# One folded product and one reciprocal for the softmax denominators of an image, and row reads of 8 KB

## The chip, the cores and the metric

The kernel runs on one core of a Trainium2 chip. The time is device time in microseconds from the first to the last instruction, as the median of several executions. One further execution was recorded by the hardware profiler, and all views of the profile are of that one.

Engines are named as in the profile: PE is TensorE, DVE is VectorE, ACT is ScalarE, POOL is GpSimd, SP is SyncE, which here issues nearly all DMAs. Each of them works through its own list of instructions in a fixed order; a wait at one instruction holds everything behind it on that engine. "PE" in the profile counts each of this kernel's matmuls twice, since each 32-bit product is recorded as two.

## What is computed

Two layers over x with 8 images, 512 channels and 32 x 32 = 1024 positions, all in 32-bit floats. The first is attention with 8 heads of 64 channels and a residual sum, the second a non-local block and a normalization over all images:

```python
q = conv1x1(x, Wq, bq); k = conv1x1(x, Wk, bk); v = conv1x1(x, Wv, bv)   # per head: 64 x 1024
attn = softmax(einsum('bhdn,bhdm->bhnm', q, k) * d ** -0.5, axis=-1)
x = x + conv1x1(einsum('bhnm,bhdm->bhdn', attn, v), Wp, bp)
...
g, theta, phi = conv1x1(x, g_w), conv1x1(x, theta_w), conv1x1(x, phi_w)
f = einsum('bcn,bdn->bcd', theta, phi) / n
z = conv1x1(einsum('bcd,bdn->bcn', f, g), W_w, W_b) + x
out = batch_normalize(z) * gamma + beta       # mean and variance over images and positions
```

The kernel computes the softmax as an exponential without a shift, a product with v, and a division by the sum of the exponentials over all 1024 keys m. The change is about that sum, the denominator: one number for each head and position, 8 x 1024 for an image.

## The kernel before, in words

**Stages.** All images go through the same stages, one after the other on TensorE: attention of image b, then q, v and k of image b+1, then the projection pp, theta and phi (ptp), g (pg), f (pf), and the product pz of image b. While TensorE computes q, v and k of the next image, VectorE finishes the denominators of the present one. The large products use seven block products in place of eight (`seven`; differences of blocks such as t1 to t4 are their operands), and q, k and pp nest the same scheme once more for two of the blocks, with results in pq_in_s, pk_in_s and pp_in_s; these are emptied one at a time by short sums on VectorE (q, k or x at L298) before their bank is used again. The last image has a shape of its own: there is no next image, so g of image 6, its f and part of its pz lie between attention and projection of image 7, and all results of earlier images are loaded back for the final normalization.

**Attention.** An image has 8 units, each a pair of heads and a half of the positions (`units`), and each unit has 8 steps, one for each block of 128 keys. A step computes scores into a bank (ps, L423), exponentials (e, L426, ScalarE), a running sum over the steps (acc, L430 and L432, VectorE: 128 key rows by 2 heads x 512 positions), and the product with v (po, L449), which lags by two steps.

**Folding.** At the end of a unit the 128 rows of acc still have to be summed. `spread` copies acc in four quarters of 32 rows into the four planes of a tile `fold` (128 x 4 x 1024), at the partitions of this unit: a group of four units fills all 128 partitions, so that three sums of 128 x 1024 (`fold_parts`, L478) reduce four units from 128 to 32 rows each. The three sums for units 0 to 3 are in the middle of attention, those for units 4 to 7 are filled in between matmuls of the next image's q (`fills` in `seven`: after its 6th, 8th and 10th matmul). There are two groups g, each in a tile of its own.

**Denominators.** `denominators(g, ps)` multiplies the folded rows by a matrix `folds` of zeros and ones (128 x 64): two matmuls (L396, one for each head of the pair) sum the 32 rows and leave each sum on 16 equal rows of a bank. A reciprocal over 128 x 512 goes back into the fold tile (L486), and all of it, 256 KB, is written to a DRAM tile den_d (L488). `normalize` reads one row of each 16 back (L497), spread to 64 partitions: four DMAs of 512 KB into a tile r. It has the same buffer as the fold tile, so it can only be filled when that has been read. Four products (L503) then scale o, in the order half by half, and within it group by group.

**Order.** The scheduler of the framework orders each engine's instructions by its own estimate, except those that the code pins in program order (`pe`, `dve`, `sp`): all matmuls, the v sums, the products with r, the fold sums of the second group, the row reads. In the seven images with a successor the order on VectorE after the q stage is: two q sums, reciprocal of group 0, two maxima of q (peak_q, L365), reciprocal of group 1, three v sums, four products with r, and then, mixed, k sums and the differences t_o (L202) that the projection uses. For the eighth image the first group's denominators are computed within attention (at step 46) and the second group's between products of g of image 6; there, `near_end` computes differences t1 to t4 of the held image 6, and calls `midway` between t2 and t3, in which `spread` copies and folds the last unit.

Of the kernel before, what the change touches and what calls it, by code (L numbers as in the profile page):

```python
# [30 lines left out]
def unshifted(ctx: ExitStack, tc: tile.TileContext, a: dict, out: bass.AP):  # L31
# [161 lines left out]
        more_sums(data, which, **how)  # L193
        return data

    def more_sums(data, which, pin=lambda ins: None, midway=lambda: None):
        for i in which:
            l, r = {1: ("12", "11"), 2: ("22", "t1"), 3: ("22", "12"), 4: ("21", "t2")}[i]
            if i == 3:
                midway()  # L200
            data[f"t{i}"] = block(f"t{i}_{data['name']}")
            pin(nc.vector.tensor_tensor(data[f"t{i}"], data[l], data[r], ALU.subtract))  # L202

# [43 lines left out]
    def seven(name, w, data, positions_out, first, add, between=None, early=False,  # L247
              by_chunk=False, inner=None, fills=()):

        nk, half = w.shape[2], w.shape[3]
        tags = list(free)
        free[:] = [tags[3], tags[1], tags[0], tags[2]] if early else [tags[3], tags[1], tags[2], tags[0]]
        slots, begun = {}, set()
        steps, done = iter(()), 0
        if inner:
            free[:] = [tags[1], tags[2], tags[3], tags[0]]
            steps = nested(name, inner, w, data, tags[2:], first, add)
        for n, (what, wi, di, s, reads) in enumerate(FIVE if inner else EARLY if early else SEVEN):  # L260
            if s not in slots or early and what == "t4":
                slots[s] = bank(tags[s], f"{name}_{s}_{n}")
                begun -= {one for one in begun if one[0] == s}
            ps, d = slots[s], data[di]
            if positions_out:
                parts = [(ps.rearrange("p h (i f) -> p (h i) f", f=half)[:, i, :], i * half // 512,
                          lambda k, i=i: d[:, k, i * P:(i + 1) * P], lambda k: w[:, wi, k, :])
                         for i in range(512 // P)]
            else:
                parts = [(ps[:, m, :], m, lambda k, m=m: w[:, wi, k, m * P:(m + 1) * P], lambda k: d[:, k, :])  # L270
                         for m in range(half // P)]
            work = [(*part, k) for part in parts for k in range(nk)]
            if by_chunk and n == 0:
                work.sort(key=lambda one: one[4])
            for to_ps, at, lhsT, rhs, k in work:
                pe(nc.tensor.matmul(to_ps, lhsT(k), rhs(k), start=(s, at) not in begun, stop=(k == nk - 1),  # L276
                                    skip_group_check=True))
                begun.add((s, at))
                if n:
                    next(steps, None)  # L280
                    done += 1
                    if done in (6, 8, 10) and fills:
                        fills[done // 2 - 3]()
            for to, is_first in reads:
                (first if is_first else add)(to, ps)
            if between and n in between:
                between[n]()
# [12 lines left out]


    xt = xp.tile([P, CC, N], F32, tag="x", name="x_0")
    warm = const.tile([P, P], F32, tag="warm", name="warm")
    nc.vector.memset(warm, 0.0)
    _, w_first = weights_tile("WqT", C // 2)
    loaded.append((queue.pop(0), w_first))
    corner["WqT"] = block("a21_WqT")[:, :, :C // 2]
# [7 lines left out]
        nc.scalar.dma_start(to[:, c0:c1], quarter("WqT", m, k)[:, c0:c1])  # L315
    ps = next_bank("warm_ps")[:, 0, :]
    for i in range(WARM):
        pe(nc.tensor.matmul(ps[:, :P], warm, warm, start=True, stop=True))
    bq, bk = load_col("bq", nc.scalar), load_col("bk", nc.scalar)
    load_w(nc.sync)  # L320

# [6 lines left out]
    nc.vector.memset(folds, 0.0)  # L328
    for i in range(4):
        nc.vector.memset(folds[i * P // 4:(i + 1) * P // 4, i * D // 4:(i + 1) * D // 4], 1.0)  # L330
    heads = const.tile([P, P], F32, tag="heads", name="heads")
    nc.vector.memset(heads, 0.0)
    for j in range(2):
        nc.vector.memset(heads[j * D:(j + 1) * D, j * D:(j + 1) * D], 1.0)
    mv = const.tile([P, CC, 2], F32, tag="mv", name="mv")
# [62 lines left out]
    def attention(b, q, k, v, near_end, make_f=None):  # L398
# [7 lines left out]
        units = [(p, h) for p in range(NPAIR) for h in range(NH)]  # L406
        steps = [(u, m) for u in range(len(units)) for m in range(NB)]
        es, accs, sums, folded, o = {}, {}, {}, {}, {}
        tags = list(free)

        def part(u):
# [3 lines left out]
        def scores(i):  # L415
            u, m = steps[i]
            p, h = units[u]
            ps = bank(tags[(0, 1, 3)[i] if i < 3 else (i + 1) % 2], f"ps_{b}_{u}_{m}")
            for j in range(2):
                r = slice(j * D, (j + 1) * D)  # L420
                for c in range(2):
                    keys = slice(m * P + c * P // 2, m * P + (c + 1) * P // 2)
                    pe(nc.tensor.matmul(ps[c * P // 2:(c + 1) * P // 2, j, :], k[r, p, keys],  # L423
                                        q[r, p, h * 512:(h + 1) * 512], start=True, stop=True, skip_group_check=True))
            e = block(f"e_{b}_{u}_{m}")
            nc.scalar.activation(e, ps, AF.Exp, scale=SCALE)  # L426
            es[u, m] = e
            if m == 1:
                accs[u] = w3.tile([P, 2, 512], F32, tag="acc", name=f"acc_{b}_{u}")
                nc.vector.tensor_tensor(accs[u], es[u, 0], e, ALU.add)  # L430
            elif m > 1:
                ins = nc.vector.tensor_tensor(accs[u], accs[u], e, ALU.add)  # L432
                if i == len(steps) - 1 and not make_f:
                    dve(ins)
            if m == NB - 1 and u == len(units) - 1 and make_f:
                near_end(lambda: spread(u, dve))
            elif m == NB - 1:
                spread(u)

# [16 lines left out]
                if i == len(steps) - 1 and not make_f:  # L456
                    dve(ins)

        def spread(u, pin=lambda ins: None):

            g, i = divmod(u, 4)
            if i == 0:
# [4 lines left out]
                eng.dma_start(folded[g][i * P // 4:(i + 1) * P // 4, k, :], acc[k * P // 4:(k + 1) * P // 4, :])  # L467
            if i == 3:
                t = folded[g]
                if g == 1 and not make_f:  # L470
                    return
                if g == 0:
                    folded[g] = fold1.tile([P, 1, 1024], F32, tag="fold1", name=f"fold1_{b}")
                for part_of in fold_parts(g, t, pin):
                    part_of()

        def fold_parts(g, t, pin):
            return [lambda to=to, l=l, r=r: pin(nc.vector.tensor_tensor(to, l, r, ALU.add)) for to, l, r in (  # L478
                (t[:, 0], t[:, 0], t[:, 1]), (t[:, 2], t[:, 2], t[:, 3]), (folded[g][:, 0], t[:, 0], t[:, 2]))]

        def denominators(g, ps):

            t = folded.pop(g)
            columns(ps, folds, lambda j: t[:, 0, j * 512:(j + 1) * 512])
            ri = t[:, 0, :512]
            nc.vector.reciprocal(ri, ps)  # L486
            d = dram2.tile([P, 512], F32, tag="den", name=f"den_d_{b}_{g}")
            nc.sync.dma_start(d, ri)  # L488
            return d

        def normalize(d):

            r = foldp.tile([P, 8, 512], F32, tag="fold", name=f"r_{b}")
            for g in range(2):
                for j in range(2):
                    rows_of = d[g].rearrange("(j i s) n -> j s i n", j=2, i=4)[j, 0]
                    sp(nc.sync.dma_start(r[j * D:(j + 1) * D, 4 * g:4 * g + 4, :], rows_of.partition_broadcast(D)))  # L497

            def products():
                for h in range(NH):  # L500
                    for g in range(2):
                        at = o["o"][:, 2 * g:2 * g + 2, h * 512:(h + 1) * 512]
                        dve(nc.vector.tensor_tensor(at, at, r[:, 4 * g + h:4 * g + 4:2, :], ALU.mult))  # L503

# [2 lines left out]
        for i in range(len(steps) + LAG):  # L507
            if i < len(steps):
                scores(i)
            if make_f and i == 2:  # L510
                make_f(bank(tags[2], f"pf_{b - 1}"))
            if not make_f and i == len(steps) - 2:
                near_end()
            if i >= LAG:
                weighted(i - LAG)
# [2 lines left out]
        free[:] = tags  # L518
        if make_f:
            return o["o"], lambda ps: denominators(1, ps), lambda d: normalize((first_den, d)), None  # L520
        return o["o"], denominators, normalize, fold_parts(1, folded[1], dve)

    def project(b, xt, o, w, between, data=None):
        def first(q, ps):
# [11 lines left out]
    def theta_phi(b, w, data, between):  # L536
# [8 lines left out]
        def first(q, ps):  # L545
            ins = nc.vector.tensor_tensor(at(q), as_tp(ps), tpb[:, int(q[0]) - 1].to_broadcast([P, NB // 2, CI]),
                                          ALU.add)
            if q == "11":
# [1 line left out]

        seven(f"ptp_{b}", w, data, True, first,
              lambda q, ps: nc.vector.tensor_tensor(at(q), at(q), as_tp(ps), ALU.add),
              {0: lambda: more_sums(data, (3, 4), pin=dve), **between})
        return tp

    def make_f(b, tp, ps):
# [81 lines left out]
    def put_away(b):  # L638

        xt, g, wf = late[b]  # L640
        for d in range(IC):
            nc.sync.dma_start(spill_g[b][:, d * N:(d + 1) * N], g[d])
        nc.sync.dma_start(spill_g[b][:, IC * N:], wf)

    def take_back(b):
        t = wr.tile([P, IC * N + IC * C], F32, tag="w", name=f"gwf_{b}")
# [93 lines left out]
    for b in range(B):  # L740
# [2 lines left out]
        if not last:  # L743
            nxt["x"] = load_x(b + 1)

        def near_end(midway=None):
            if last:
                nxt["data"] = data_sums(quarters_of(held["x"]), f"x1_{b - 1}_again", pin=dve, midway=midway)
            else:
                nxt["data"] = data_sums(quarters_of(nxt["x"]), f"x_{b + 1}", (1, 2))  # L750

        def held_f(ps):
            held["f"] = make_f(b - 1, held["tp"], ps)
# [3 lines left out]
        if not last:  # L757
# [2 lines left out]
            q, peak_q = heads_of(b + 1, "q", weights("WqT"), bq, nxt["data"], dve, inner="WqT",  # L760
                                 between={1: lambda: inner_sums(nxt["data"], "t4", dve)}, fills=last_fold)
            load_w(nc.sync)
            d = [denominators(g, next_bank(f"den_{b}_{g}")[:, 0, :]) for g in range(2)]
            v = values(b + 1, weights("WvT"), nxt["data"], {5: normalize(d)})
            load_w(nc.sync)

# [27 lines left out]
        if b == B - LATE:  # L794
            for cc in range(CC):
                nc.sync.dma_start(spill[b][:, cc, :], xt[:, cc, :])
        data = data_sums(quarters_of(xt), f"x1_{b}", (1, 2))
        if last:
            reload_chunks(B - LATE)
        elif b > B - LATE and b != B - 2:  # L800
# [241 lines left out]
```

## Time and profile before

| | us |
|---|---|
| median of 3 executions | 2181.84 (2181.07 to 2182.1) |
| the profiled execution | 2181.89 |
| its span, first to last instruction | 2180.1 |
| mean granted TensorE clock | 0.993 |
| scores ps and product po (L423, L449), on the chain | 20% each |
| ptp, pp, pv, pq, pk, pg (L276), on the chain | 9, 7, 7, 6, 6, 4% |
| denominator products den (L396), 64 records | 15.7 busy |
| reciprocals (L486), 16 of 128 x 512 | 53.6 busy, 3350 ns each |
| fold sums (L478), 48 of 128 x 1024 | 58.7 busy, 1222 ns each |
| VectorE idle before the products with r, for the DMA of r | 36.8 in 8 places |
| copies fold<-acc, 128 KB each, issue to landing | 2.3 median, 2.0 to 4.3 |
| writes den_d<-fold, 256 KB each | 2.5 median |
| reads r<-den_d, 512 KB each | 9.8 median, 5.6 to 15.1 |

The span is the stretch between the first and the last recorded instruction; the execution's own time is 1.8 us longer. Busy times of different engines overlap and don't add up to the span. The chain is what the profiler follows back from the last instruction, at each step to what released it; a share of the chain is a share of the span. In a timeline row the columns are start in us, duration in us (of all instructions merged in the row), engine, line, operation, output<-input with shapes, count, and in brackets the idle time just before and what ended it. In a list of waits they are engine and line, what was waited for, and then us in total, times, and the longest.

### The profile page before, as it was taken

To read this page: it belongs to the slowest core of one execution; us is meant where nothing else is said; L and a number is where in the kernel's file an instruction comes from. 1 tells how busy PE (TensorE), PEld (TensorE's weight loads), DVE (VectorE), ACT (ScalarE), POOL (GpSimd) and SP (SyncE) were. 2 spreads that over 40 slices of the span, in tenths; PEclk is the share of its full clock that TensorE was granted. 3 is DMA by queue.
4 is the path that set the end of the run, shared out by engine and by line. 5 is a ranking of instruction groups with operands and counts; after the bars stand their busy time and mean duration, and the time that the engine had idled before them with its cause. 6 is when DMAs were issued, how large, how long until landed. Compare 5 with 4: busy or idle time off the path is not lost.

```text
span 2180.1 us, 29638 instructions
## 1 busy us (share of the span) xinstructions
PE 2142.0 (98%) x12454; PEld 1109.4 (51%) x12454; DVE 1423.3 (65%) x1612; ACT 741.5 (34%) x848; POOL 45.1 (2%) x50
## 2 busy tenths in 40 slices
PE   9999999999999999999999999999999999999896
PEld 4534663356733566336563366533665346733362
DVE  6477656776477764777747767467673777568626
ACT  1463104631046310562106621165203641065015
POOL 0000100000000000000000000000000000000000
PEclk9999999999999999999999999999999999999998
DMA  6312433124131232313323132231424115111739
GB/s 215 133 38 62 127 150 130 40 66 118 68 131 40 77 108 101 108 40 84 99 93 107 40 103 97 111 81 39 132 99 153 40 30 158 57 40 39 262 127 358
DMA packets 58893, 223.40 MB, mean 102 GB/s; under 512 B 9344, under 2 KB 15744, under 8 KB 53248
## 3 DMA queue, kind: packets, MB, share of 16 engines
q1 hardware_dynamic: 57264, 220.11, 31.8%
q8 instruction: 100, 1.64, 0.3%
q10 hardware_dynamic: 1488, 1.32, 0.2%
q14 instruction: 41, 0.34, 0.0%
HBM read 138.03 MB, written 49.81 MB: 86 GB/s over the span
## 4 chain that ended last, share of the span: by engine, by line
PE 93%; DMA 2%; DVE 2%; issue 1%; ACT 1%; SPq 0%; DVEq 0%
PE ps L423 20%; PE po L449 20%; PE ptp L276 9%; PE pp L276 7%; PE pv L276 7%; PE pq L276 6%; PE pk L276 6%; PE pg L276 4%; PE pf L561 3%; PE pz L276 2%; PE pk_in_s L239 2%; PE pq_in_s L239 2%; PE pp_in_s L239 2%; PE pz L671 2%; DMA r<-den_d 1%; PE pwf L596 1%
## 5 line engine op out<-in xcount | busy, mean ns | idle before, releaser
L426 ACT ACTIVATE e<-ps 128x1024 f32<-128x1024 f32 x512 | 522.9, 1025 | 427.9 <-PE ps L423 422.4
L432 DVE TENSOR_TENSOR acc<-acc,e 128x1024 f32<-128x1024 f32 x384 | 470.0, 1224 | 129.3 <-ACT e L426 121.6
L449 PE MATMUL po<-e,v 64*64 64x512 f32 x4096 | 528.7, 589 | 0.7 <-ACT w_WgT L563 0.7
L423 PE MATMUL ps<-q,k 64*64 64x512 f32 x4096 | 529.1, 589 | 0.0
L449 PEld LDWEIGHTS po<-e,v 64*64 64x64 f32 x4096 | 156.5, 133 | 283.4 <-issue 275.4
L423 PEld LDWEIGHTS ps<-q,k 64*64 64x64 f32 x4096 | 155.6, 133 | 284.1 <-issue 275.0
L584 ACT ACTIVATE g<-pg,gb 128x512 f32<-128x512 f32 x31 | 21.3, 687 | 398.8 <-PE pg L276 395.9
L430 DVE TENSOR_TENSOR acc<-e,e 128x1024 f32<-128x1024 f32 x64 | 78.2, 1222 | 108.7 <-ACT e L426 73.4
L276 PE MATMUL ptp<-w_tp,t_x 128*128 128x256 f32 x512 | 116.7, 384 | 2.4 <-DVE t_x L202 2.4
L276 PE MATMUL pv<-w_WvT,t_x 128*128 128x256 f32 x512 | 114.5, 379 | 0.0
L276 PEld LDWEIGHTS ptp<-w_tp,t_x 128*128 128x128 f32 x512 | 97.8, 192 | 16.1 <-DVE t_x L202 2.9
L276 PEld LDWEIGHTS pv<-w_WvT,t_x 128*128 128x128 f32 x512 | 97.2, 190 | 13.2
L276 PE MATMUL pp<-t_o,w_WpT 128*128 128x512 f32 x208 | 100.9, 592 | 0.0
L276 PE MATMUL pq<-t_x,w_WqT 128*128 128x512 f32 x200 | 98.8, 593 | 0.9 <-DVE w_WqT L723 0.9
L276 PE MATMUL pk<-t_x,w_WkT 128*128 128x512 f32 x200 | 98.9, 592 | 0.0
L379 ACT COPY v<-pv 128x1024 f32<-128x1024 f32 x32 | 32.4, 1012 | 191.2 <-PE pv L276 191.2
L276 PE MATMUL pv<-w_WvT,x 128*128 128x256 f32 x384 | 87.5, 381 | 0.0
L276 PE MATMUL ptp<-w_tp,x 128*128 128x256 f32 x384 | 86.8, 379 | 0.0
L380 DVE TENSOR_TENSOR v<-v,pv 128x1024 f32<-128x1024 f32 x24 | 29.3, 1222 | 79.9 <-PE pv L276 79.9
L276 PEld LDWEIGHTS pv<-w_WvT,x 128*128 128x128 f32 x384 | 72.4, 190 | 15.7 <-issue 5.9
L276 PEld LDWEIGHTS ptp<-w_tp,x 128*128 128x128 f32 x384 | 73.0, 190 | 13.3 <-issue 3.6
L276 PE MATMUL pp<-o,w_WpT 128*128 128x512 f32 x144 | 70.1, 611 | 7.8 <-issue 5.2
(181 smaller groups left out, 2200.4 us busy)
## 6 DMA issues: line engine op xcount, KB each, us to landing
fold<-acc SPq DMA_DIRECT2D x254, 128.0 KB, 2.3
r<-den_d SPq DMA_DIRECT2D x32, 512.0 KB, 9.8
x<-in_x_dram SPq DMA_DIRECT2D x31, 512.0 KB, 6.1
w_WqT<-kept_WqT SPq DMA_DIRECT2D x7, 2176.0 KB, 8.8
w_WkT<-kept_WkT SPq DMA_DIRECT2D x7, 2176.0 KB, 8.3
w_WpT<-kept_WpT SPq DMA_DIRECT2D x6, 2176.0 KB, 8.9
w_WvT<-kept_WvT SPq DMA_DIRECT2D x7, 1792.0 KB, 7.2
w_tp<-kept_tp SPq DMA_DIRECT2D x7, 1792.0 KB, 7.4
```

The lines of the kernel that those rows point to most:

```text
L239: pe(nc.tensor.matmul(ps, a[wi], d[di], start=s not in begun, stop=True, skip_group_check=True))
L276: pe(nc.tensor.matmul(to_ps, lhsT(k), rhs(k), start=(s, at) not in begun, stop=(k == nk - 1), skip_group_check=True))
L379: seven(f"pv_{b}", w, data, True, lambda q, ps: nc.scalar.copy(at(q), as_v(ps)), lambda q, ps: dve(nc.vector.tensor_tensor(at(q), at(q), a ...
L380: lambda q, ps: dve(nc.vector.tensor_tensor(at(q), at(q), as_v(ps), ALU.add)), between)
L423: pe(nc.tensor.matmul(ps[c * P // 2:(c + 1) * P // 2, j, :], k[r, p, keys], q[r, p, h * 512:(h + 1) * 512], start=True, stop=True, skip_gr ...
L426: nc.scalar.activation(e, ps, AF.Exp, scale=SCALE)
L430: nc.vector.tensor_tensor(accs[u], es[u, 0], e, ALU.add)
L432: ins = nc.vector.tensor_tensor(accs[u], accs[u], e, ALU.add)
L449: pe(nc.tensor.matmul(ps[j * D:(j + 1) * D, r, :], v[keys, m, (2 * p + j) * D:(2 * p + j + 1) * D], e[keys, j, :], start=(m == 0), stop=(m ...
L561: pe(nc.tensor.matmul(ps[:, c, :], tp[:, i, c * P:(c + 1) * P], tp[:, i, CI:], start=(i == 0), stop=(i == NB - 1)))
L596: pe(nc.tensor.matmul(ps, f[:, c, d * P:(d + 1) * P], ww[:, c, :], start=(c == 0), stop=(c == IC - 1)))
L671: pe(nc.tensor.matmul(ps[:, h - h0, :], wf[:, d, oc * P:(oc + 1) * P], g[d][:, h * 512:(h + 1) * 512], start=(d == 0), stop=(d == IC - 1), ...
```

## The change

For the seven images with a successor, the three fold sums of the second group stay where they were (`fold_last`: after the 6th, 8th and 10th matmul). With the last of them, four DMAs on SP's queue copy the 32 rows of each unit of both groups into two planes of the fold tile, every other row into each (64 rows of 4 KB a copy), and after the 14th matmul a further sum adds the two planes: all eight units now lie on the 128 partitions with 16 rows each. `all_denominators` needs one product of two matmuls with a new matrix `folds8`, one reciprocal, and one write of 16 rows of 2 KB: one row for each sum. These rows are laid out so that the four rows that a partition of r needs follow each other, 8 KB in one piece.

For the last image the two groups keep their own products and reciprocals. The second reciprocal goes into another tile (`ri`), the rows of group 0 are read as soon as the second product is done, and the writes are of 8 rows each. t1 and t2 of the held image are computed during attention (after steps 59 and 61), t3 and t4 while the last copies of acc are under way.

The products with r now run group by group. In the last image all four differences of x1 are made before ptp. `heads` takes the place of `warm` for the warm-up matmuls and is filled with its ones afterwards; `folds8` is built on GpSimd; for image 6 the writes of `put_away` are pinned in SP's order.

```diff
     def seven(name, w, data, positions_out, first, add, between=None, early=False, by_chunk=False, inner=None, fills=()):
...
-                    if done in (6, 8, 10) and fills:
-                        fills[done // 2 - 3]()
+                    if done in fills:
+                        fills[done]()
...
+    folds8 = const.tile([P, D], F32, tag="folds8", name="folds8")
+    nc.gpsimd.memset(folds8, 0.0)
+    nc.gpsimd.affine_select(out=folds8, in_=folds8, compare_op=ALU.is_gt, fill=1.0, base=1 - P // 8,
+                            pattern=[[-P // 8, 8], [0, D // 8]], channel_multiplier=1)
+    nc.gpsimd.affine_select(out=folds8, in_=folds8, compare_op=ALU.is_ge, fill=0.0, base=0,
+                            pattern=[[-P // 8, 8], [0, D // 8]], channel_multiplier=1)
...
             if m == NB - 1 and u == len(units) - 1 and make_f:
-                near_end(lambda: spread(u, dve))
+                spread(u, dve, near_end)
...
             if i == 3:
                 t = folded[g]
+                meanwhile()
                 if g == 1 and not make_f:
                     return
...
+        def fold_last():
+
+            t = folded.pop(1)
+            folded["all"] = t[:, 1]
+            adds = [lambda to=to, l=l, r=r: dve(nc.vector.tensor_tensor(to, l, r, ALU.add)) for to, l, r in (
+                (t[:, 0], t[:, 0], t[:, 1]), (t[:, 2], t[:, 2], t[:, 3]), (t[:, 0], t[:, 0], t[:, 2]),
+                (t[:, 1], t[:, 1], t[:, 2]))]
+            first = folded.pop(0)[:, 0]
+
+            def last_of_group():
+                adds[2]()
+                for g, rows_32 in enumerate((first, t[:, 0])):
+                    for half in range(2):
+                        nc.sync.dma_start(t[g * D:(g + 1) * D, 1 + half, :],
+                                          rows_32.rearrange("(r s) n -> s r n", s=2)[half])
+
+            return {6: adds[0], 8: adds[1], 10: last_of_group, 14: adds[3]}
...
+        def all_denominators(ps):
+
+            t = folded.pop("all")
+            columns(ps, folds8, lambda j: t[:, j * 512:(j + 1) * 512])
+            ri = t[:, :512]
+            nc.vector.reciprocal(ri, ps)
+            d = dram2.tile([16, 512], F32, tag="den", name=f"den_d_{b}")
+            nc.sync.dma_start(d, ri.rearrange("(a s) n -> a s n", a=16)[:, 0, :])
+            d = d.rearrange("(j g i) n -> g j (i n)", j=2, g=2)
+            return d[0], d[1]
+
         def denominators(g, ps):
...
-            ri = t[:, 0, :512]
+            alone = make_f and g == 1
+            ri = (fold1.tile([P, 1, 1024], F32, tag="fold1", name=f"ri_{b}") if alone else t)[:, 0, :512]
             nc.vector.reciprocal(ri, ps)
-            d = dram2.tile([P, 512], F32, tag="den", name=f"den_d_{b}_{g}")
-            nc.sync.dma_start(d, ri)
-            return d
+            if alone:
+                rows_of(0, first_den)
+            d = dram2.tile([8, 512], F32, tag=f"den{g}", name=f"den_d_{b}_{g}")
+            nc.sync.dma_start(d, ri.rearrange("(a s) n -> a s n", a=8)[:, 0, :])
+            return d.rearrange("(j i) n -> j (i n)", j=2)
+
+        def rows_of(g, d):
+            if "all" not in rows:
+                rows["all"] = foldp.tile([P, 8, 512], F32, tag="fold", name=f"r_{b}")
+            rows[g] = rows["all"][:, 4 * g:4 * g + 4, :].rearrange("q i n -> q (i n)")
+            for j in range(2):
+                sp(nc.sync.dma_start(rows[g][j * D:(j + 1) * D, :], d[j].partition_broadcast(D)))
 
         def normalize(d):
 
-            r = foldp.tile([P, 8, 512], F32, tag="fold", name=f"r_{b}")
             for g in range(2):
-                for j in range(2):
-                    rows_of = d[g].rearrange("(j i s) n -> j s i n", j=2, i=4)[j, 0]
-                    sp(nc.sync.dma_start(r[j * D:(j + 1) * D, 4 * g:4 * g + 4, :], rows_of.partition_broadcast(D)))
+                if g not in rows:
+                    rows_of(g, d[g])
+            r = rows["all"]
 
             def products():
-                for h in range(NH):
-                    for g in range(2):
+                for g in range(2):
+                    for h in range(NH):
...
-            if not make_f and i == len(steps) - 2:
+            if i in ((len(steps) - 5, len(steps) - 3) if make_f else (len(steps) - 2,)):
                 near_end()
...
-            d = [denominators(g, next_bank(f"den_{b}_{g}")[:, 0, :]) for g in range(2)]
+            d = denominators(next_bank(f"den_{b}")[:, 0, :])
...
-        data = data_sums(quarters_of(xt), f"x1_{b}", (1, 2))
+        data = data_sums(quarters_of(xt), f"x1_{b}", (1, 2, 3, 4) if last else (1, 2))
```

## Prediction, made before the changed kernel ran

> **What bounds the kernel.** I read the page's shares and its chain of waits first, then the waits of TensorE alone, then the timeline of the stages that the diff touches.
>
> ```profile
> PE 2142.0 (98%) x12454; PEld 1109.4 (51%) x12454; DVE 1423.3 (65%) x1612; ACT 741.5 (34%) x848; POOL 45.1 (2%) x50
> ...
> PE 93%; DMA 2%; DVE 2%; issue 1%; ACT 1%; SPq 0%; DVEq 0%
> ...
> PE pp L276 <- issue: 5.2, 1, 5.2
> PE pk_in_s L239 <- DVE k L298: 3.0, 2, 2.2
> PE pp L276 <- DVE o L503: 2.6, 1, 2.6
> PE ptp L276 <- DVE t_x L202: 2.4, 1, 2.4
> ```
>
> TensorE is busy for 98% of the span and carries 93% of the chain; its own waits sum to about 16 us. So time comes out in two ways only: fewer matmuls, or fewer of those few waits. VectorE at 65% costs nothing except where TensorE waits for it. Fewer reciprocals are therefore worth nothing by themselves (16 x 3350 ns is all VectorE time), and I look for the waits they feed.
>
> **1. One product for the denominators (seven images).** On the chain each image has its denominators as one piece; the last image shows one group alone.
>
> ```profile
> 480.86 1.87 PE den L396 x8
> ...
> 1982.70 1.01 PE den L396 x4
> ```
>
> Two groups take 1.87 us, one takes 1.01 (x4 is two matmuls, each recorded twice). The new product has the shape of one group: 1.87 - 1.01 = 0.86 us off TensorE, and nothing lies beside it. Seven images: **-6.0 us** (0.78 to 0.93 each, depending on how the first weight load is hidden). The eighth keeps two separate products.
>
> **2. What the product now waits for.** A new round trip stands before it: fold sums, four copies SBUF to SBUF (64 rows of 4 KB, 256 KB each), one more 128x1024 sum, product. In the second image:
>
> ```profile
> 470.67 2.48 DVE L478 TENSOR_TENSOR fold<-fold 128x1024 f32<-128x1024 f32 x2
> 478.40 2.34 DVE L365 TENSOR_REDUCE peak_q<-q 128x1 f32<-128x1024 f32 x2
> 480.79 1.94 PE L396 MATMUL den<-fold,folds 128*64 128x512 f32 x8
> ```
>
> The last sum ends at 473.15. Four issues of about 0.6 us follow on SP, where nothing else waits until the WkT load at 480.89. The trace has no 256 KB copy inside SBUF; its nearest row is fold<-acc, 128 KB in rows of 4 KB: 2.3 us median, 4.3 at most. I take 2.5, so the last copy lands at 477.5 (478.7 at worst). VectorE's static order puts the added sum between the two peak_q reductions. The first starts at 478.40 and the issue interval is 1.13, so the sum runs 479.53 to 480.76. TensorE reaches the product at 480.79: just in time, with a hand-over on top. I charge 0.1 us per image, **+0.7** (0 to 1.5). Behind the waiting sum stand a reduction, two sums that empty a bank of q, and the reciprocal; the bank's next use is late in the v stage, some 17 us on, so their delay of 1.1 us costs nothing. If the copies land after 479.5, every microsecond costs one per image.
>
> **3. The rows come earlier.** Now the second reciprocal starts at 488.63, after two reductions, and the rows are issued at 494.24. With one reciprocal, at 484.1 to 487.4, a 32 KB write in place of two of 256 KB (2.5 us) puts the reads at about 489.9. In most images the late rows are hidden; in the fourth they were not:
>
> ```profile
> 1035.65 1.22 DVE L503 TENSOR_TENSOR o<-o,r 128x1024 f32<-128x1024 f32 x1
> ...
> 1043.10 3.50 DVE L503 TENSOR_TENSOR o<-o,r 128x1024 f32<-128x1024 f32 x3 [6.24 <-DMA r<-den_d]
> ...
> 1046.52 0.41 DVE L298 TENSOR_TENSOR k<-k,pk_in_s 128x256 f32<-128x256 f32 x1
> ...
> 1046.99 0.70 PE L239 MATMUL pk_in_s<-i_x,w_WkT 128*128 128x256 f32 x2 [2.19 <-DVE k L298]
> ```
>
> VectorE sits 6.24 us in its queue for the rows, the k sums behind it are late, and TensorE stops. By the starts on the chain this k stage takes 1037.76 to 1064.12 = 26.36 us, the five others between 23.2 and 23.5 (772.57 to 795.83, for one): 3.1 lost. In the first image it is 238.27 to 264.08 = 25.81, of which 0.81 is the bias product at 263.13: 1.8 lost. The order after puts three t_o differences ahead of the first k sum. From the v sum at 1034.51: eight operations at 1.14 us put the k sum at +9.1, while TensorE needs it at +9.8 (1046.52 - 2.19 - 1034.51). Tight, but clear by 0.7 if the rows are there. In the first image the order also puts weight sums there, which need loads issued when v ends. I take 3.1 whole and 1.4 of 1.8: **-4.5** (2 to 5).
>
> Are the rows there? The old reads landed up to 15.1 us after issue (5.6 to 15.1). 489.9 + 15.1 = 505.0 meets the second group's product, now third in order, at 503.9 + 2.3 - 0.9 = 505.3: enough even with no faster reads. The Trainium skill speaks against the 8 KB rows (*DMA: Bandwidth & Descriptors*, section "Why small descriptors are slow"): the bus overhead is some three cycles per packet. Its arithmetic at 2 KB gives an estimate of 3/67, about 4%, so four times longer packets would leave 15 us at 14.5. The trace says otherwise: while the 2 KB rows run, the window from 496 to 507 has 171 GB/s at a DMA share of 0.86; just before, with the 17 KB rows of a weight, the DMA view shows 429. I lean to the trace, perhaps 8 us, but the sum is the same by both: the earlier issue does the work.
>
> **4. The last image: projection.** Here the rows are waited for openly.
>
> ```profile
> 2028.35 0.33 SPq L488 DMA_DIRECT2D den_d<-fold  x1
> 2030.60 3.75 SPq L497 DMA_DIRECT2D r<-den_d  x4
> 2039.91 1.23 DVE L503 TENSOR_TENSOR o<-o,r 128x1024 f32<-128x1024 f32 x1 [9.00 <-DMA r<-den_d]
> 2041.24 5.88 PE L276 MATMUL pp<-o,w_WpT 128*128 128x512 f32 x8 [5.18 <-issue]
> 2047.16 1.41 DVE L530 SCALAR_TENSOR_TENSOR x<-pp,bp,x 128x512 f32<-128x512 f32 x2 [6.02 <-PE pp L276]
> 2049.76 3.70 PE L276 MATMUL pp<-o,w_WpT 128*128 128x512 f32 x8 [2.63 <-DVE o L503]
> ```
>
> TensorE stops at 2036.06, and its first eight records take 5.88 us instead of the usual 3.6, since the window 2040 to 2050 has a granted clock of 0.72. After: the first group's rows are read as soon as the second product has freed the fold buffer, about 2023.4 (its reciprocal no longer writes into it), and land by 2031 at the old pace. Both first-group products come before the second group's. So pp starts when the matmuls before it end (2035.9, with the 0.2 wait at pwf also gone) and takes 3.5, to 2039.4. Then the order has two x sums ahead of the second group's products: 2 x 0.66 + 1.2, so the second eight still wait 2.6, now to 2041.9 instead of 2049.76: **-7.85**. The second rows are no limit: reciprocal over at 2026.9 (two differences no longer ahead of it), reads at 2029.1, landed by 2037.
>
> That wait of 2.6 may cost clock. The skill (*TensorE: Matmul & The Clock Gate*, section "Why this matters for your kernels") lets idle gaps of up to about 3 us pass free. The trace has 2.63 without a drop and 2.45 (at ptp, below) followed by half clock. I take the row: about one chance in two of losing 1.7, **+0.95**; by the rule nothing.
>
> **5. The last image: ptp.**
>
> ```profile
> 2085.61 1.22 DVE L202 TENSOR_TENSOR t_x<-x 128x1024 f32<-128x1024 f32 x1
> 2086.75 1.22 DVE L202 TENSOR_TENSOR t_x<-x,t_x 128x1024 f32<-128x1024 f32 x1
> 2086.89 5.27 PE L276 MATMUL ptp<-w_tp,t_x 128*128 128x256 f32 x16 [2.45 <-DVE t_x L202]
> 2092.00 3.62 PE L276 MATMUL ptp<-w_tp,x 128*128 128x256 f32 x16
> ```
>
> The differences t3 and t4 move ahead of the tp sums, into the first 3.5 us of ptp. The wait goes, 2.45, and with it the half clock: sixteen records took 5.11 instead of 3.45. **-4.1** by the row (2.45 by the skill's rule). The first tp sum moves from 2074.11 to 2075.4; its bank is wanted at 2077.4. Nothing is late next.
>
> Edits at nothing: t1 and t2 of the held image inside attention (2.3 us of VectorE, which idles 0.49 in each 1.72 us step); POOL's three instructions for folds8 (2% busy); the second memset of heads, behind a weight sum at 8.25 us, long after the warm-up at 4.7. Uncovered, each costs its own length, at most 2.3 once.
>
> **Sum.** -6.0 + 0.7 - 4.5 - 7.85 + 0.95 - 4.1 = -20.8. The profiled execution took 2181.89 us, the median is 2181.84: **2161 us**, 1% faster. Behind this the output tail follows TensorE; weight and spill loads have slack (DMA share 0.74 and 0.50 after 2060).
>
> **Rivals.**
> *The last image gives little* (0.20): another wait takes the place, the first rows land late, or ptp waits elsewhere. For it: four kinds of DMA meet there, and the windows from 2040 to 2060 show a DMA share of 1.02. Against: rows are issued before all of it. -20.8 + 11 leaves -10: 2172.
> *Small waits in every image* (0.10): product or k sum late by 0.5 to 1 us, on the thin margins of 0 and 0.7 us above: 7 x 0.8 = 5.6, 2167.
> *Slower* (0.04): the copies of part 2 land late. They pay from 6.4 us after the sums; 3 us more per image eats all 20.8, so it decides at about 9.4. At 10.4, near the rows' median of 9.8, each image loses 4 us and mostly a half-clock window of 1.7: 7 x 5.7 = 40, 2201. The 2.3 and 4.3 of fold<-acc speak against it.
> *No change* (0.02): the saved matmuls turn into waiting and the last image fails too: about 2180.
> The forecast has 0.64, its own range 2157 to 2165. With the next two: **2156 to 2170**. A measurement tells apart 0.2%, 4.4 us: faster 0.94, same 0.02, slower 0.04.
>
> **What would show it.** Right: den x4 on each image's chain with no wait before it; both k stages near 23.3; no wait for r on VectorE before the last image; pp after pz without a gap, then one of 2.6; no wait at ptp. Wrong: TensorE waiting at den for the fold sum, or at pk_in_s in images that ran clean.

## The result, and the profile after

The changed kernel takes 2171.47 us (median of 6, 2170.06 to 2172.12), the kernel before on the same chip 2182.16 us (median of 6): ratio 0.995, interval 0.9937 to 0.9963. It is faster by 10.7 us, where 20.8 were forecast, and 1.5 us above the range. Small waits in every image, one of the rivals, were what happened, at twice the size given there; their cause, copies that land late, stood under another rival, *Slower*.

The page after, shares and chain, and below it the waits of TensorE alone (engine, line, what for, us in total, times, longest):

```profile
PE 2131.9 (98%) x12426; PEld 1108.3 (51%) x12426; DVE 1411.2 (65%) x1611; ACT 741.6 (34%) x848; POOL 44.1 (2%) x53
...
PE 98%; issue 1%; DVE 1%; ACT 1%
...
PE den L398 <- issue: 11.4, 7, 1.8
PE pp L274 <- DVE o L545: 2.6, 1, 2.6
```

Of the four waits that the prediction lists, only the 2.6 us at pp is left, and one line is new: TensorE waits 11.4 us in seven places for the new product, 1.6 an image. That is the whole distance to the forecast. The view calls it "issue", which only says that it could not name the releaser. The rows of VectorE and SP in the second image show what it was (timeline of the kernel after):

```profile
469.47 4.52 SPq L494 DMA_DIRECT2D fold<-fold  x4
469.69 2.48 DVE L485 TENSOR_TENSOR fold<-fold 128x1024 f32<-128x1024 f32 x2
477.42 1.21 DVE L367 TENSOR_REDUCE peak_q<-q 128x1 f32<-128x1024 f32 x1
480.14 1.23 DVE L485 TENSOR_TENSOR fold<-fold 128x1024 f32<-128x1024 f32 x1 [1.51 <-DMA fold<-fold]
481.47 1.08 PE L398 MATMUL den<-fold,folds 128*64 128x512 f32 x4 [1.58 <-issue]
```

The fold sums end at 472.17 and the copies behind them have landed at 480.14. VectorE was free from 478.63 and TensorE from 479.88. The product follows the added sum by 0.1 us, so its 1.58 us are the copies' lateness, handed on. The data view from 469 to 481 us (columns of 0.3 us; busy share of the DMA engines in tenths, then GB/s) shows why they are late:

```profile
DMA  0000069950000059979987988996998200000009
GB/s 0 0 0 0 0 246 396 164 68 0 0 0 0 0 205 423 177 96 164 137 109 109 191 96 123 137 137 82 150 164 96 27 0 0 0 0 0 0 0 522
```

While the copies run the engines are busy nearly all the time, but after a fast start they move only some 130 GB/s. By the trace's own packets (4 KB each), the quickest quarter takes 156 to 168 ns and the slowest half 458 to 641. It isn't a fixed time to land either: the four copies land 3.8, 4.2, 5.6 and 6.7 us after their issues. The queue is full, and slow.

The rest came as forecast. Both k stages that had lost time now take what the others take (starts on the chain after, first and fourth image; the first has its bias product of 0.79 in it):

```profile
239.10 4.29 PE pk L274 x10
...
263.09 24.14 PE pp L274 x56
...
1039.28 4.29 PE pk L274 x10
...
1062.49 4.29 PE pp L274 x10
```

That is 23.99 and 23.21 us, against 25.81 and 26.36 before.

### The profile page after: what moved, and what is told of

The parts are those of the page before. It is cut to its first block, busy times and chain, and to the rows that moved or that the text cites. A ratio compares the mean times of both kernels' runs of the same rounds, so it can differ in the third digit from the quotient of the medians.

```text
span 2169.5 us, 29636 instructions
## 1 busy us (share of the span) xinstructions
PE 2131.9 (98%) x12426; PEld 1108.3 (51%) x12426; DVE 1411.2 (65%) x1611; ACT 741.6 (34%) x848; POOL 44.1 (2%) x53
## 4 chain that ended last, share of the span: by engine, by line
PE 98%; issue 1%; DVE 1%; ACT 1%
PE ps L426 20%; PE po L452 20%; PE pv L274 9%; PE ptp L274 9%; PE pp L274 7%; PE pq L274 7%; PE pk L274 7%; PE pg L274 4%; PE pf L603 3%; PE pz L274 2%; PE pq_in_s L237 2%; PE pk_in_s L237 2%; PE pp_in_s L237 2%; PE pz L714 2%; PE pwf L638 1%
## 5 line engine op out<-in xcount | busy, mean ns | idle before, releaser
L274 PEld LDWEIGHTS pv<-w_WvT,t_x 128*128 128x128 f32 x512 | 97.2, 190 | 13.2
L274 PEld LDWEIGHTS ptp<-w_tp,x 128*128 128x128 f32 x384 | 73.0, 190 | 13.3 <-issue 3.6
```

## The experiments

All start from the changed kernel. Times are medians, and a ratio is to the kernel before, run beside it. With the short labels below, that kernel took 2179.9 us beside e1, e2, e3 and e4, 2179.5 beside e3b, e5, e7 and b3, and 2177.8 beside e8 and e9, so totals of different groups compare to some 2 us only, and the waits in the traces are the finer measure.

**Fewer bytes at the end (e1).** The copies of group 0 leave earlier, into planes 1 and 3 (`with_copies` makes a sum, then issues the copies that are named).

```diff
-                (t[:, 1], t[:, 1], t[:, 2]))]
+                (t[:, 1], t[:, 1], t[:, 3]))]
...
-            return {6: adds[0], 8: adds[1], 10: last_of_group, 14: adds[3]}
+            return {6: with_copies(0, (0, first, 0)), 8: with_copies(1, (0, first, 1)),
+                    10: with_copies(2, (1, t[:, 0], 0), (1, t[:, 0], 1)), 14: adds[3]}
```

> Only the place of the copies changes: those of group 0 go into planes 1 and 3 of the fold tile right after the 6th and 8th fill, so that after the last fold sum only 512 KB are still to be copied, in place of 768. Theory A (the copies are slow by their bytes, about 131 GB/s): they are over 2 us earlier, the wait of the product falls from 1.6 us to under 0.2 in each of seven images, 7 x 1.5 = 10.5 less than the change: 2161. Theory B (a copy inside SBUF lands a fixed 6 us after its issue): the last copy is still issued after the last sum, only 0.5 us earlier; the wait stays at 1.0 or more: 2167 to 2169.

Measured: 2166.31 us, ratio to before 0.9936 (0.992 to 0.9953). The wait fell to 0.9 us an image (4.4 in five, 2.1 in two), between the two forecasts. Theory B falls, since the copies land 4.2, 4.8, 5.5 and 6.7 us after their issues. Theory A had the rate too high. By the packets of the second image, the two copies of group 1 are under way from 473.28 to 477.70 us, 512 KB at 119 GB/s. And the 256 KB that are no longer at the end would have been the quick ones: of the three last copies of the change the first takes 1.4 us from first to last packet, the other two 2.4 each.

**Same bytes, other partitions (e2).** A copy's rows go to every second partition of all 128; `folds2` is `folds8` with its rows exchanged to match. Theory A1 below is that the destination's partitions set the rate.

```diff
-                        nc.sync.dma_start(t[g * D:(g + 1) * D, 1 + half, :],
+                        nc.sync.dma_start(t[:, 1 + half, :].rearrange("(r g) n -> g r n", g=2)[g],
                                           rows_32.rearrange("(r s) n -> s r n", s=2)[half])
...
+    folds2 = const.tile([P, D], F32, tag="folds2", name="folds2")
+    for g in range(2):
+        nc.sync.dma_start(folds2.rearrange("(r g) n -> g r n", g=2)[g], folds8[g * D:(g + 1) * D, :])
```

> Same four copies, same bytes, same time of issue, but a copy's 64 rows go to every second partition of all 128 instead of to 64 neighbouring ones (the matrix of ones has its rows exchanged to match). Theory A1[...]: 1 MB moves at 250 GB/s or more, the added sum finds its data, no wait at the product: 2161. Theory A2 (the rate belongs to 4 KB rows copied within SBUF, wherever they go) and B (fixed time to land): wait of 1.6 us per image as before, 2171.5.

Measured: 2159.93 us, ratio 0.9905 (0.9888 to 0.9921). No wait at the product. The data view of this run, same window:

```profile
DMA  8930000008999997000000000000000000990367
GB/s 341 410 123 0 0 0 0 0 0 314 396 369 423 410 423 287 0 0 0 0 0 0 0 0 0 0 0 0 0 0 0 0 0 0 519 290 0 116 232 290
```

Some four hundred GB/s, and every 4 KB packet of this image's four copies takes 156 to 176 ns. In the timeline the added sum follows the reduction without idle time, and the product follows q:

```profile
475.86 1.21 DVE L370 TENSOR_REDUCE peak_q<-q 128x1 f32<-128x1024 f32 x1
476.99 1.22 DVE L488 TENSOR_TENSOR fold<-fold 128x1024 f32<-128x1024 f32 x1
478.12 1.21 DVE L370 TENSOR_REDUCE peak_q<-q 128x1 f32<-128x1024 f32 x1
478.31 1.08 PE L401 MATMUL den<-fold,folds 128*64 128x512 f32 x4
```

So the rate, and with it the 11 us, hangs on which partitions the copies touch, and neither on the bytes alone nor on a fixed time: the four copies land after 2.3 to 2.4 us.

**Which side of the copy (e9).** Source rows that are neighbours, destination as in the change. This kernel leaves out the right pairing of rows, so it serves for the times alone.

```diff
-                                          rows_32.rearrange("(r s) n -> s r n", s=2)[half])
+                                          rows_32[half * D:(half + 1) * D])
```

> The copies take 64 neighbouring rows in place of every other one, to 64 neighbouring partitions as in the change; the sums then mix the rows of two units, so the denominators are not those of the reference. Theory A1 (the destination's 64 neighbours set the rate): the copies stay at some 131 GB/s and the product waits 1.6 us. Rival (the source's step of two partitions has a part in it): the rate is clearly other than 131 GB/s; [...]the copies are over 2 us earlier and the wait is under 0.3.

Measured, one execution: 2158.84 us, no wait at the product. The data view, from 468 to 480 us:

```profile
DMA  0000999920000899968999983000000000000099
GB/s 0 0 0 0 218 205 191 191 68 0 0 0 0 205 218 205 177 150 246 355 273 287 259 178 68 0 0 0 0 0 0 0 0 0 0 0 0 0 635 290
```

The median packet takes 316 ns. My theory that the 64 neighbours at the destination alone set the rate has fallen. Three pairs of patterns gave three rates. From first to last packet, the three copies behind the fold sums (768 KB) took in the second image 2.1 us from every second partition to every second (375 GB/s), 3.6 from neighbours to neighbours (221), and 5.5 from every second to neighbours (144, with the fast start). So neighbours on both sides cost two fifths of the rate, and spreading only the source made it worse. The Trainium skill (*SBUF — State Buffer*, section "Door 1: The DMA port swizzle") says that DMA bandwidth depends on how many of 16 ports the partitions reach, and by its formula 64 neighbouring partitions reach 8: an estimate of half of its 436 GB/s, 218. That fits the second pair and not the third, and the measurement decides. What makes the third slower still was not tried, nor was the fourth pair, neighbours to every second.

**The product later (e3, e3b).** TensorE goes on with v first. `make_denominators` holds the product, the reciprocal and the reads; its key says behind which block of v it stands.

```diff
-            d = denominators(next_bank(f"den_{b}")[:, 0, :])
-            v = values(b + 1, weights("WvT"), nxt["data"], {5: normalize(d)})
+            v = values(b + 1, weights("WvT"), nxt["data"], {0: make_denominators, 5: lambda: scale["o"]()})
```

> The copies stay as slow as in the change, but TensorE comes to the product 3.4 us later, after the first block of v. Theory A and B alike: the copies land meanwhile, no wait on TensorE, and the rows still arrive in time: 2171.5 - 7 x 1.6 = 2160.5. Rival (the delay of the added sum on VectorE is what costs, by q sums and banks that come free late): TensorE waits elsewhere in v, and most of the 11 us stays, 2167 to 2171.

Measured: 2171.19 us, ratio 0.9956 (0.9939 to 0.9972): nothing gained. The product waits 1.5 us again, though TensorE now comes to it 3.6 us later:

```profile
480.31 1.22 DVE L485 TENSOR_TENSOR fold<-fold 128x1024 f32<-128x1024 f32 x1 [1.52 <-DMA fold<-fold]
481.45 1.21 DVE L367 TENSOR_REDUCE peak_q<-q 128x1 f32<-128x1024 f32 x1
482.58 2.34 DVE L296 TENSOR_TENSOR q<-q,pq 128x1024 f32<-128x1024 f32 x2
485.02 1.08 PE L398 MATMUL den<-fold,folds 128*64 128x512 f32 x4 [1.53 <-issue]
```

Its data had been there since 481.5. It starts 0.1 us after the two q sums end, which stand behind the late sum on VectorE. By the order in which the code hands out banks (`next_bank`), the product was given, at this place, the bank that they read. The next run moves it one more block on:

```diff
-            v = values(b + 1, weights("WvT"), nxt["data"], {0: make_denominators, 5: lambda: scale["o"]()})
+            v = values(b + 1, weights("WvT"), nxt["data"], {1: make_denominators, 5: lambda: scale["o"]()})
```

> In the run before, TensorE came to the product 3.4 us later and waited all the same, until the q sums that stand behind the added sum on VectorE had emptied the bank that the product was given. Here the product comes one block of v later still, 6.9 us after the end of q, and those sums are over by then. If the bank was the cause: no wait at the product, 2171.5 - 7 x 1.6 = 2160.5. If it is something that moves along with the product, a wait of 1.5 us stays, 2171.

Measured: 2159.94 us, ratio 0.9906 (0.9889 to 0.9923), no wait at the product, though VectorE still stands 10.5 us in seven places for copies as slow as ever. The lateness costs only where TensorE meets it. Slow copies hidden are worth as much as fast ones.

**Two products again (e4).** The seven images as before, with the compact rows and the new order of the products with r.

```diff
-            d = denominators(next_bank(f"den_{b}")[:, 0, :])
+            d = [denominators(g, next_bank(f"den_{b}_{g}")[:, 0, :]) for g in range(2)]
...
-            return {6: adds[0], 8: adds[1], 10: last_of_group, 14: adds[3]}
+            return {6: adds[0], 8: adds[1], 10: adds[2]}
```

> The seven images get two products and two reciprocals again, without copies and added sum; row layout, 8 KB reads, order of the products and the last image stay as changed. If the single product with its wait is a loss as it stands (1.57 + 1.08 = 2.65 us against 1.87): 2171.5 - 7 x 0.78 = 2166, faster than the change. If the 4.5 us that the first and fourth image gained came from the single reciprocal, they return: 2170, with waits at pk_in_s. If they came from faster reads as well, they stay away.

Measured: 2165.12 us, ratio 0.9932 (0.9915 to 0.9949), no wait at pk_in_s. The folding that gives the change its name was a loss of 6 us as it stood, 0.8 an image. And the first and fourth image keep their gain with two reciprocals. An earlier issue is not the reason here: the reads leave 13.0 to 13.2 us after the product starts, before the change 13.3 to 14.3. What differs is that their last packet ends 10.9 to 11.9 us after the first issue, before 14.0 to 16.8, and that the products with r take group 1 third and not second. The two were not tried apart.

**The row reads (e5, e8).** Pieces of 2 KB again, first 4 KB apart, then 32 KB as before the change (the number of rows in den_d and the 2 below become 16 times the written rows and 16).

```diff
-            d = dram2.tile([16, 512], F32, tag="den", name=f"den_d_{b}")
+            d = dram2.tile([32, 512], F32, tag="den", name=f"den_d_{b}")
+            d = d.rearrange("(a s) n -> a s n", s=2)[:, 0, :]
...
-                sp(nc.sync.dma_start(rows[g][j * D:(j + 1) * D, :], d[j].partition_broadcast(D)))
+                sp(nc.sync.dma_start(rows[g][j * D:(j + 1) * D].rearrange("q (i n) -> q i n", i=4), d[j].partition_broadcast(D)))
```

> The changed kernel with the rows of r read in pieces of 2 KB again, as many bytes and DMAs, issued at the same time. Theory of the prediction (the earlier issue does the work, not the size of a piece): the reads may land later than the 6.8 us median of the change, but VectorE meets at most a short wait for them in the last image, and the time stays at 2171.5 within 1.5. Rival (8 KB pieces are what removed the wait): waits for r of some 5 us on VectorE and waits at pk_in_s return, 2174 to 2178.

> The pieces of 2 KB that make up a row of r now lie 32 KB apart in DRAM, as they did before the change (4 KB apart in the run with 2 KB pieces, which read as fast as 8 KB pieces did). If the distance made the old reads slow: median from issue to landing near the 9.8 us of before and a longest one near 15. If it was what else was under way at the time: 7 to 7.5 median, 11 at most, as in the run with 2 KB pieces. Time in both cases 2171.5 within 2.

Measured: 2171.43 us (ratio 0.9958, 0.9941 to 0.9974) with 4 KB between the starts of pieces, 2172.3 in one execution with 32 KB. Shortest, median and longest time of a read from issue to landing, in the kernels before and after and in these two:

| | piece | apart | us |
|---|---|---|---|
| before | 2 KB | 32 KB | 5.6 / 9.8 / 15.1 |
| after | 8 KB | 2 KB | 4.5 / 6.8 / 10.4 |
| first run | 2 KB | 4 KB | 5.0 / 7.2 / 10.7 |
| second run | 2 KB | 32 KB | 5.6 / 8.3 / 15.3 |

(For the kernel after, "apart" is the distance of the rows that make up one piece.) The size of a piece is worth little, 6.8 against 7.2 us; the distance in DRAM carries the long tail. It accounts for the old reads: in the seven images whose four reads leave together, the fourth lands after 12.7 to 15.1 us before the change, 9.8 to 10.4 after it, 10.0 to 10.7 in the first run and 12.5 to 15.3 in the second. (The medians 9.8 and 8.3 differ because the last image of the changed kernels reads two by two.) Neither shows in the time, since the reads now start early enough, 8.5 us after the product in most images: the run with 32 KB has only 2.8 us of waits for r on VectorE in all, and TensorE waits where it does in the change, to 0.4 us.

**The last image, ptp (e7).** t3 and t4 go back behind the tp sums.

```diff
-        data = data_sums(quarters_of(xt), f"x1_{b}", (1, 2, 3, 4) if last else (1, 2))
+        data = data_sums(quarters_of(xt), f"x1_{b}", (1, 2))
```

> The changed kernel with t3 and t4 of x1 in the last image left where they were before, behind the sums of tp. Theory: the wait at ptp comes back, 2.45 us, and if its 3.4 us window of the clock is mostly idle another 1.7: 2174 to 2176. Rival (VectorE is ahead by now and the wait does not return): 2171.5.

Measured: 2174.11 us, ratio 0.9974 (0.9962 to 0.9985), 2.6 above the change. That alone is little more than totals can tell; the trace has the wait again, and this time without half clock:

```profile
2080.83 3.72 PE L274 MATMUL ptp<-w_tp,t_x 128*128 128x256 f32 x16 [2.45 <-DVE t_x L200]
2084.39 3.62 PE L274 MATMUL ptp<-w_tp,x 128*128 128x256 f32 x16
```

Sixteen records take 3.56 us from start to start; before the change, after the same wait of 2.45, they took 5.11.

**The best version (b3).** Copies to every second partition, and in the last image the first x sums of pp behind the products with r.

```diff
-                nc.vector.scalar_tensor_tensor(at, ps[:, m, :], bp[:, c:c + 1], at, ALU.add, ALU.add)
+                ins = nc.vector.scalar_tensor_tensor(at, ps[:, m, :], bp[:, c:c + 1], at, ALU.add, ALU.add)
+                if b == B - 1 and q == "11":
+                    dve(ins)
```

> The copies to every second partition as in the second experiment, and in the last image the two x sums of the first block of pp pinned behind the four products with r. Theory: the wait of 2.6 us at the second block of pp goes, and with it the window at half clock behind it: 2160 - 2.6 - 1.7 = 2155.7. Rival (the second group's rows land later than TensorE needs them, so the wait stays): 2159 to 2160.

Measured: 2156.21 us (2156.05 to 2156.43), ratio 0.989 (0.9874 to 0.9907). The wait at the second block of pp is down to 0.3:

```profile
2027.38 2.36 DVE L548 TENSOR_TENSOR o<-o,r 128x1024 f32<-128x1024 f32 x2 [3.86 <-DMA r<-den_d]
2028.66 3.70 PE L274 MATMUL pp<-o,w_WpT 128*128 128x512 f32 x8 [0.31 <-DVE o L548]
```

VectorE waits 3.86 us for the second group's rows here, and it costs TensorE 0.31, since it falls under the first block. This kernel beats the change by 15 us and the one before by 23.

## Why the prediction was wrong

**The failed step is the second, "what the product now waits for".** It put the last copy's landing at 477.5 us, "478.7 at worst", and charged 0.1 us an image. TensorE reaches the product 0.9 us earlier after the change; by that clock the copies were due at 476.6, and they were there at 480.1. I had taken the landing of one copy of 128 KB and added the time to issue four of 256 KB. (With the row's longest landing of 4.3 us that sum gives 479.3, not 478.7: next to no margin before 479.5.) But the four queue behind each other, and what counts is their sum. Three of them come after the last fold sum: their 768 KB were under way for 5.5 us, with 1.2 us before the first packet and 1.3 behind the last, 8.0 in all; to every second partition the same bytes took 2.1. The row that I called nearest said so in another view: in the trace of before, four copies of 128 KB to 32 partitions each keep the engines at a mean of about 200 GB/s, with a median packet of 307 ns, about twice the shortest of the change. I read the time to landing and not the rate. The skill's page quoted above would have warned at half the rate.

Point by point, with the spans of the two profiled executions (2180.1 and 2169.5 us, 10.6 less):

| step | forecast | measured | from |
|---|---|---|---|
| 1, one product | -6.0 | -5.5 | 7 x (1.08 - 1.87), starts on the chain |
| 2, its wait | +0.7 | +11.4 | the list of waits |
| 3, k stages of two images | -4.5 | -5.0 | -1.8 and -3.15 |
| 4, pp of the last image | -7.85 | -8.3 | pg's start to pp's second block: 35.06 and 26.76 us |
| 4, half clock behind its wait | +0.95 | +1.4 | rest of pp: 20.70 and 22.09 us |
| 5, ptp of the last image | -4.1 | -4.3 | 28.44 and 24.18 us |
| sum | -20.8 | -10.3 | |

- *Step 2, the point of decision.* That a late landing pays from 6.4 us after the sums, one for one in each image, was right. It landed at 7.97.
- *Step 3.* The gain was right and its reason half right. One reciprocal is not needed for it: with two reciprocals and compact rows it stays. "The earlier issue does the work" holds for the run with pieces 32 KB apart, where the reads are as slow as before; the run with two products shows that quicker reads, with the new order of the products, do it too. On the size of a piece I leaned to the trace against the skill's rule of a few cycles a packet, and the rule was nearer: 6.8 and 7.2 us. The slow rate that I had read off came with the distance of 32 KB, which the row did not show.
- *Step 4.* The reordered products and the early reads did what was said: pp starts 20.5 us after pg (21.2 forecast) and its second block 26.8 after it (27.2). The remaining wait, read off the static order, was 2.63. It cost half clock, as charged at one chance in two. The window after it (its length, the busy times of PE, PEld, DVE, ACT and POOL, then granted clock, DMA share and GB/s):

```profile
2041.30:2044.80 3.50, 2.85 (x4) 1.30 (x5) 3.47 (x4) 0.00 (x0) 0.00 (x0) 0.51 0.95 388
```

  The 0.51 is the granted clock. So gaps under 3 us are not always free, against the skill's guideline quoted in the prediction; but the run on ptp shows the same gap of 2.45 without a drop. The traces say when. In all twelve, the stretches of full and half clock within the kernel last whole multiples of 3.41 us. Lay that step over each trace, from some 11 us to the last matmul: half clock follows all 10 steps in which TensorE is idle for 2.00 us or more, and none of the 42 with 1.00 to 1.98. The wait of 2.63 put 2.05 us into one step after the change and, split by a boundary, 1.98 before it; at ptp the 2.45 gave 2.21 before and 1.08 and 1.37 in the run with t3 and t4 back. So the drop here was a matter of where the wait fell: 7 of the 11 traces with this wait have it. This is read off the traces; no run set out to test it.
- *The edits at nothing* cost nothing that shows: no wait of TensorE before the last image other than at the product and two that were there before, 1.1 us at the warm-up matmuls and 0.7 at po.
- *The range* missed because the margin of nothing at the product was known ("just in time") but its bounds were drawn from one narrow row.

## What to carry to other kernels

When copies are put between two steps of a busy engine, price them by what queues together divided by a rate measured for that pattern of partitions, not by the landing of one. Copies within SBUF that touched 64 neighbours ran here at 0.6 or 0.4 of the rate of those that had every second partition on both sides; spread both sides, or give the engine that waits something else to do first, past any bank that the delay holds. An engine that is saved work but made to wait for longer loses: here the halved product lost 6 us until its wait was removed.

## What the runs showed that I had not expected

- 768 KB in 4 KB rows from partition to partition within SBUF, 64 rows a DMA, took 2.1 us from every second partition to every second, 3.6 from neighbours to neighbours and 5.5 from every second to neighbours, with the DMA engines busy nearly all the time in each case (packets of 161, 316 and 458 ns in the median).
- Reads that spread DRAM rows to 64 partitions, four of 512 KB together: the last lands after 10.7 us at most when its pieces of 2 KB start 4 KB apart, and after 12.5 to 15.3 when they start 32 KB apart.
- A wait of 2.63 us on TensorE was followed by 3.41 us at half clock in seven traces and not in four; what told them apart was whether 2.00 us or more of it fell into one step of 3.41 us.
